# Sorting networks on VectorE: leaving idle lanes in their buffer instead of copying them at every step

## The chip, the cores and the metric

The kernel runs on one core of one Trainium2 chip. The metric is the device time of one execution in microseconds (us); lower is better. The engines are named as in the profile: PE (TensorE), DVE (VectorE), ACT (ScalarE), POOL (GpSimd) and SP (SyncE, which issues transfers).

## The reference

Sixteen graphs of 1024 nodes with 64 channels go through four layers, each with a layer norm and a ReLU ahead and a residual behind: a dense graph product, an attention layer, a hyperbolic attention layer, and a last layer that matters here. Cut to that:

```python
nd = adj_d > 0                                   # neighbours left after a thinning of the graph
vals = jnp.where(nd[..., None], x[:, None, :, :], jnp.inf)
s = jnp.sort(vals, axis=2)                       # per node and channel, over the neighbours
nv = nd.sum(2)
for tau, w in zip((0.25, 0.5, 0.75), (0.25, 0.5, 0.25)):
    pos = tau * maximum(nv - 1, 0)
    lo, hi, frac = floor(pos), ceil(pos), pos - floor(pos)
    agg = agg + w * (s[lo] + frac * (s[hi] - s[lo]))
out = x + agg
y = (relu(out @ W1 + b1) @ W2 + b2) * mask
```

So for each node and channel a weighted sum of three quantiles over the node's neighbours is wanted, which takes a sort of a few to some 288 values per node and channel.

## The kernel before, in words

The nodes of a graph are ranked by how many neighbours they have. The 80 with the most are **hubs**. They are sorted with channels (of two nodes at a time) on the 128 partitions and all their neighbours side by side in one row of 2736 values, cut into segments of 288, 192, 128, 96, 64, 48 and 40 lanes (`HUB`, `HUB_OFF`). The others, **lows**, have a node on each partition and 31 to 7 neighbours of 64 channels each in the row (`LOW`, seven groups per graph). Both sort by a Batcher network of comparators: a step takes the maximum and the minimum of pairs of lanes at a distance `k`, two DVE instructions for each regular set of pairs.

A step doesn't work in place. It reads one buffer and writes the other: `ha` and `hb` for the hubs, `la` (where gathered rows land) and `lb` for the lows. The next step swaps them. A lane that no comparator of a step touches, an idle lane, is therefore copied from one to the other by ACT, so that the next step finds all its lanes in one place. In `step` and `first` (hubs) the idle lanes come from `comparators`; in `sort_low` they are the set `stay` that `network` gives for each step. `lanes` and `at` make the strided views, `stretches` turns a set of lanes into regular runs.

`sort_hub` calls `step` for the networks of width 2, 4, 8, 16, 32 on all segments at once, then for the wider merges on the longer segments alone, with `first` where a segment isn't a power of two. `finish_hub` runs the sort and then multiplies the sorted lanes by weights that pick the quantiles and adds them up (`aggh`). `lows` does the same for each group (`aggl`).

What runs beside it are several Python generators, one for each kind of work: `heads` (layers 0 to 2 and the norm of layer 3), `places` (the thinning and the ranking: activations `d`, comparisons `rem`, casts `ng` and `vr`), `weigh`, `fetches` (the search for neighbours and the gathers by POOL into `la` and `hg`), `hubs`, `lows` and `finish`. A planner in Python (`Plan`, `Stream`) books a cost for every instruction, keeps a due time per generator from DVE time (`HEADS_US`, `HUBS_US`, `LOWS_US`) and picks whose next piece is emitted. The class `Queue` then fixes the order on every engine: each engine runs its instructions exactly in the order in which they were emitted, and a later one never overtakes one that waits. Nearly every instruction carries line 187 in the profile, the line of that helper, so groups are told apart by tile names.

Of the kernel before, what the change touches and what calls it, by code (L numbers as in the profile page):

```python
# [57 lines left out]
HUB_OFF = {}  # L58
# [200 lines left out]
def network(d, needed):  # L259


    out = []
    for st in reversed(batcher(d)):
        act = [c for c in st if needed & set(c)]
        both = {e for c in act for e in c}
        stay = needed - both
        out.append((st[0][1] - st[0][0], [a for a, _ in act if a in needed], [b for _, b in act if b in needed], stay))
        needed = stay | both
    assert needed == set(range(d))
    return out[::-1]  # L270
# [23 lines left out]
def tile_gnn_stack(  # L294
# [1525 lines left out]
    def comparators(D, p, k):  # L1820


        if k == p:
            runs = [(0, 1, D - p)]
        else:
            full = max(0, (D - 2 * k) // (2 * k) + 1) if D >= 2 * k else 0
            full = min(full, p // k - 1)
            while full and k + 2 * k * (full - 1) + 2 * k > D:
                full -= 1
            runs = [(k, full, k)] if full else []  # L1830
            part = D - (k + 2 * k * full) - k
            if full < p // k - 1 and part > 0:
                runs.append((k + 2 * k * full, 1, min(part, k)))
        used = set()
        for j0, m, w in runs:
            for g in range(m):
                for i in range(w):
                    used |= {j0 + 2 * k * g + i, j0 + 2 * k * g + i + k}
        idle, j = [], 0
        while j < D:  # L1840
            e = j
            while e < D and e not in used:
                e += 1
            if e > j:
                idle.append((j, e))
            j = max(e, j + 1)
        return runs, idle

    def lanes(buf, off, n, st, j, m, w, step):

        v = buf[:, off + j:off + j + n * st].rearrange("p (n d) -> p n d", d=st)
        if m == 1:
            return v[:, :, 0:w]
        return v[:, :, 0:m * step].rearrange("p n (m s) -> p n m s", s=step)[:, :, :, 0:w]

    def compare(hi, lo, a, b):
        nc.vector.tensor_tensor(hi, a, b, ALU.max)
        nc.vector.tensor_tensor(lo, a, b, ALU.min)

    def step(src, dst, p, k, blocks):  # L1860


        for so, do, n, st, D in blocks:
            idle = comparators(D, p, k)[1]
            if len(idle) == 2 and idle[0][1] - idle[0][0] == idle[1][1] - idle[1][0] and idle[1][0] <= st // 2:
                idle = [(*idle[0], 2, idle[1][0] - idle[0][0])]
            for j, e, *r in idle:
                m, stp = r or (1, 0)
                nc.scalar.copy(lanes(dst, do, n, st, j, m, e - j, stp), lanes(src, so, n, st, j, m, e - j, stp))
        for so, do, n, st, D in blocks:  # L1870
            for j, m, w in comparators(D, p, k)[0]:
                a, b = (lanes(src, so, n, st, j + o, m, w, 2 * k) for o in (0, k))
                for o, op in ((0, ALU.max), (k, ALU.min)):
                    nc.vector.tensor_tensor(lanes(dst, do, n, st, j + o, m, w, 2 * k), a, b, op)
                    yield []

    def first(dst, a, b, n, p, D):

        r = D - p
        av, bv = lanes(*a[:2], n, a[2], 0, 1, p, 0), lanes(*b[:2], n, b[2], 0, 1, r, 0)  # L1880
        dv = lanes(*dst[:2], n, dst[2], 0, 1, D, 0)
        compare(dv[:, :, 0:r], dv[:, :, p:D], av[:, :, 0:r], bv)
        if r < p:
            nc.scalar.copy(dv[:, :, r:p], av[:, :, r:p])

    def same(o, n, d, D=None):
        return (o, o, n, d, D or d)
# [1 line left out]
    def sort_low(a, b, pn, nt, d, needed):  # L1889

        def at(buf, j, m, st, w):
            v = buf[:pn].rearrange("p t l c -> p t (l c)")
            if m == 1:
                return v[:, :, j * C:(j + w) * C]
            o = j if j + m * st <= d else j - (st - w)
            assert o >= 0
            return v[:, :, o * C:(o + m * st) * C].rearrange("p t (m s) -> p t m s", m=m)[:, :, :, (j - o) * C:(j - o + w) * C]

        def parts(lanes, *offs):
            for j, m, st, w in stretches(lanes):  # L1900
                fits = m == 1 or all(j + o + m * st <= d or j + o >= st - w for o in offs)
                yield from [(j, m, st, w)] if fits else [(j, m - 1, st, w), (j + (m - 1) * st, 1, w, w)]

        for k, hi, lo, stay in network(d, set(needed)):
            for j, *r in parts(hi, 0, k):
                nc.vector.tensor_tensor(at(b, j, *r), at(a, j, *r), at(a, j + k, *r), ALU.max)
            for j, *r in parts(lo, 0, -k):
                nc.vector.tensor_tensor(at(b, j, *r), at(a, j - k, *r), at(a, j, *r), ALU.min)
            for j, *r in parts(stay, 0):
                nc.scalar.copy(at(b, j, *r), at(a, j, *r))  # L1910
            a, b = b, a
            yield
        return a

    def sort_hub(a, b):

        o40, o48, o64, o192, o128, o288, o96 = (HUB_OFF[c] for c in HUB_ORDER)
        s, d = a, b
        n40, n48 = (next(h[1] for h in HUB if h[2] == c) for c in (40, 48))
        for p in (1, 2, 4, 8, 16):  # L1920
            k = p
            while k:
                if p < 8:
                    yield from step(s, d, p, k, [same(0, HUB_N // (2 * p), 2 * p)])
                elif p < 16:
                    yield from step(s, d, p, k, [same(o40 + 16 * h, n40, 40, 16) for h in range(2)] + [same(o48, (HUB_N - o48) // 16, 16)])
                else:
                    yield from step(s, d, p, k, [same(o40, n40, 40, 32), same(o48, n48, 48, 32), same(o64, (HUB_N - o64) // 32, 32)])
                s, d, k = d, s, k // 2
                yield  # L1930
        first((a, o40, 40), (b, o40, 40), (a, o40 + 32, 40), n40, 32, 40)
        first((a, o48, 48), (b, o48, 48), (a, o48 + 32, 48), n48, 32, 48)
        n64 = (HUB_N - o64 - 6 * 96) // 64
        yield from step(b, a, 32, 32, [same(o64, n64, 64), same(o96, 6, 96, 64)])
        s, d, k = a, b, 16
        while k:
            yield
            yield from step(s, d, 32, k, [same(o40, n40, 40), same(o48, n48, 48), same(o64, n64, 64), same(o96, 6, 96, 64)])
            s, d, k = d, s, k // 2
        k = 64  # L1940
        while k:
            yield
            yield from step(s, d, 64, k, [same(o192, 1, 192, 128), same(o128, 4, 128), same(o96, 6, 96)])
            s, d, k = d, s, k // 2
        yield
        first((b, o192, 192), (a, o192, 192), (b, o192 + 128, 192), 1, 128, 192)
        yield from step(a, b, 128, 128, [same(o288, 1, 288, 256)])
        s, d, k = b, a, 64
        while k:
            yield  # L1950
            yield from step(s, d, 128, k, [same(o192, 1, 192), same(o288, 1, 288, 256)])
            s, d, k = d, s, k // 2
        yield
        first((b, o288, 288), (a, o288, 288), (b, o288 + 256, 288), 1, 256, 288)
        s, d, k = b, a, 128
        while k:
            yield
            yield from step(s, d, 256, k, [same(o288, 1, 288)])
            s, d, k = d, s, k // 2

    class Tail:
# [224 lines left out]
        def finish_hub(self, graph, a, b, wd):  # L2186
            wp = self.wp
            aggh = self.sums[graph, 0] = self.bp.tile([P, HQ], F32, name="aggh", bufs=2)
            yield from sort_hub(a, b)
            w = wp.tile([P, HUB_N], F16, tag="wb", name="wb", bufs=1)  # L2190
            for h in range(2):
                nc.sync.dma_start(w[64 * h:64 * h + 64, :], wd[h].partition_broadcast(64))
            yield
            yield [w]
            for q0, nq, cap, few in HUB:
                o, l0, l1 = HUB_OFF[cap], (few - 1) // 4, -(-3 * (cap - 1) // 4) + 1
                v, wv = (u[:, o:o + nq * cap].rearrange("p (n l) -> p n l", l=cap)[:, :, l0:l1]
                         for u in (a if cap in (192, 128, 96) else b, w))
                nc.vector.tensor_tensor(v, v, wv, ALU.mult)
                nc.vector.tensor_reduce(aggh[:, q0:q0 + nq], v, AX.X, ALU.add)  # L2200
            yield []
# [202 lines left out]
```

## Time and profile before

| what | value |
|---|---|
| runs of the kernel | 5921.93, 5931.84, 5931.37 us, median 5931.37 us |
| profiled execution | 6619.39 us, span 6617.5 us |
| mean granted TensorE clock in the profiled execution | 0.61 |
| DVE busy | 5113.9 us, 13,854 instructions in the record |
| ACT busy | 3432.8 us, 10,163 instructions |
| POOL busy | 3586.6 us, 2,903 instructions |
| PE busy | 3205.6 us, 13,232 matmuls |
| hub sort on DVE, `hb<-ha` and `ha<-hb` | 640.9 + 606.8 us, 1632 + 1568 instructions |
| low sort on DVE, `lb<-la` and `la<-lb` | 677.6 + 695.4 us, 1760 + 1856 instructions |
| copies of idle lanes on ACT, hubs | 273.2 + 255.8 us, 1280 + 1264 instructions |
| copies of idle lanes on ACT, lows | 300.5 + 223.3 us, 944 + 768 instructions |

The profile is of one execution, which took longer than the unprofiled runs; busy times and waits in it are compared with its own span. A group's row gives the tile written, the tile read, the number of instructions, their busy time and the mean of one, and then the engine's idle time ahead of them with what ended it. "PE granted clock" is a mean over the span. Some matmul records can be missing.

### The profile page before, as it was taken

The page shows a single profiled execution, that of the slowest core. Times are in us where ns is not written, and L with a number is a line of the kernel's source. Part 1 is how long each engine was busy: PE and PEld are TensorE (multiplying, and loading weights), DVE is VectorE, ACT ScalarE, POOL GpSimd, SP SyncE. Part 2 cuts the span into 40 slices and gives each one's busy share as a digit, 9 for nine tenths or more (in the row PEclk, how much of TensorE's full clock was granted, in tenths as well). Part 3 has the DMA queues.
Part 4 walks back from the last instruction along what each step waited for, and adds up shares of the span by engine and source line. Part 5 has one row for each costly group of instructions (what it writes and reads, how often), then busy time and mean ns, then how long its engine had stood idle before and what let it go on. Part 6 is the DMA issues. An engine that isn't in the chain of part 4 may idle for free. (4 is left out here: it accounts for less than half of the span.)

```text
span 6617.5 us, 61215 instructions
## 1 busy us (share of the span) xinstructions
PE 3205.6 (48%) x13232; PEld 1794.6 (27%) x13233; DVE 5113.9 (77%) x13854; ACT 3432.8 (52%) x10163; POOL 3586.6 (54%) x2903
## 2 busy tenths in 40 slices
PE   6554463645636445453545635346363645535310
PEld 2223232322413223231322413224132332313200
DVE  3568687795978869787796878869687796877957
ACT  5355464554656455564554646455464654645523
POOL 0263564655546564664646646465564546646576
PEclk7656556566655656655566656656566566665655
DMA  2221322222222222322223222222222222222121
GB/s 65 80 55 51 83 58 69 63 78 62 60 70 67 65 57 57 92 55 61 64 56 84 61 62 71 66 61 58 79 60 73 56 68 73 62 59 71 42 42 19
DMA packets 460786, 419.44 MB, mean 63 GB/s; under 512 B 218067, under 2 KB 351667, under 8 KB 460404
## 3 DMA queue, kind: packets, MB, share of 16 engines
q1 hardware_dynamic: 353908, 295.94, 15.6%
q0 software_dynamic: 106496, 119.49, 9.1%
q14 instruction: 275, 2.25, 0.1%
q8 instruction: 107, 1.75, 0.1%
HBM read 363.99 MB, written 50.54 MB: 63 GB/s over the span
## 5 line engine op out<-in xcount | busy, mean ns | idle before, releaser
L187 POOL DMA_INDIRECT la<-s_hd,ix x1856 | 2364.3, 1274 | 2144.2 <-DVE ix L187 1067.8
L187 POOL DMA_INDIRECT hg<-s_hd,ix x768 | 949.6, 1236 | 358.9 <-issue 275.7
L187 DVE TENSOR_TENSOR lb<-la 128x128 f32<-128x128 f32 (+14 forms) x1760 | 677.6, 436 | 269.2 <-ACT la L187 181.9
L187 DVE TENSOR_TENSOR la<-lb 128x256 f32<-128x256 f32 (+11 forms) x1856 | 695.4, 430 | 133.3 <-ACT lb L187 99.5
L187 DVE TENSOR_TENSOR ha<-hb 128x64 f32<-128x64 f32 (+36 forms) x1568 | 606.8, 441 | 174.8 <-ACT hb L187 122.5
L187 DVE TENSOR_TENSOR hb<-ha 128x128 f32<-128x128 f32 (+36 forms) x1632 | 640.9, 447 | 91.0 <-ACT ha L187 67.0
L187 PE MATMUL pv<-wtile,krow 8*128 8x512 f16 x512 | 292.6, 572 | 597.5 <-ACT d L187 299.7
L187 PE MATMUL pw<-ident,u_z 128*128 128x128 f32 x1024 | 236.8, 376 | 463.0 <-DVE u_z L187 358.2
L187 ACT COPY lb<-la 128x64 f32<-128x64 f32 (+11 forms) x944 | 300.5, 354 | 219.2 <-issue 76.7
L187 PE MATMUL pm<-w,hn 128*65 128x128 f32 x2048 | 404.7, 380 | 6.8 <-DVE w L187 6.8
L187 PEld LDWEIGHTS <-ng 128*128 128x128 f16 x2048 | 169.5, 126 | 818.9 <-issue 818.9
L187 ACT ACTIVATE d<-pv,n_mid 128x512 f16<-128x512 f32 x256 | 174.0, 688 | 419.4 <-remote 261.1
L187 PEld LDWEIGHTS pm<-w,hn 128*65 128x65 f32 x2048 | 388.3, 210 | 10.0 <-DVE w L187 9.9
L187 PE MATMUL pd<-tab_r,tab_dist 67*128 67x512 f32 x512 | 373.6, 821 | 25.7 <-DVE u_g L187 18.0
L187 POOL DMA_INDIRECT s_vp<-vr,s_place x128 | 134.8, 1053 | 433.7 <-DVE c_sb L187 142.6
L187 ACT ACTIVATE u_g<-pd,gxc 128x512 f32<-128x512 f32 x256 | 174.1, 680 | 365.4 <-PE pd L187 199.2
L187 PE MATMUL pl<-tab_ll,tab_rl 66*128 66x512 f32 x512 | 360.8, 795 | 0.0
L187 PEld LDWEIGHTS pw<-ident,u_z 128*128 128x128 f32 x1024 | 170.8, 193 | 674.3 <-issue 593.4
L187 PE MATMUL pf<-vcol,one 128*1 128x3 f32 x32 | 3.1, 166 | 664.5 <-DVE vcol L187 664.5
L187 PE MATMUL pa<-adj,h 128*64 128x512 f32 x512 | 199.8, 909 | 251.2 <-DMA adj<-in_adjt 117.6
L187 ACT COPY ha<-hb 128x4 f32<-128x4 f32 (+22 forms) x1264 | 255.8, 269 | 123.6 <-DVE hb L187 101.5
L187 ACT COPY hb<-ha 128x32 f32<-128x32 f32 (+24 forms) x1280 | 273.2, 284 | 79.6 <-DVE ha L187 65.9
(342 smaller groups left out, 8647.0 us busy)
## 6 DMA issues: line engine op xcount, KB each, us to landing
adj<-in_adjt SPq DMA_DIRECT2D x384, 512.0 KB
la<-s_hd,ix POOLq DMA_INDIRECT x1856
row<-s_vp SPq DMA_DIRECT2D x112, 256.0 KB
hg<-s_hd,ix POOLq DMA_INDIRECT x768
wb<-wd SPq DMA_DIRECT2D x32, 342.0 KB
row<-s_vp SPq DMA_DIRECT2D x192, 28.0 KB
row<-s_vp SPq DMA_DIRECT2D x192, 24.0 KB
xa<-in_x SPq DMA_DIRECT2D x16, 256.0 KB
```

The source lines that it names most:

```text
L187: r = f(*a, **k)
```

## The change

All sorts keep a record of where each lane is. A lane that a step leaves alone stays in the buffer it is in. Where the next step that reads it reads the other buffer, it is copied, once, at the first step at which it is idle; where that step reads the same buffer, it isn't copied.

For the lows this is worked out in `sort_low` from the list of steps: `where` holds the buffer of each lane, `reads` the lanes that each step reads (the last entry being those wanted at the end). The copies are also emitted ahead of the step's comparators and no longer after them. For the hubs a new class `Sort` with one instance `hs` does it in two passes: the first time, `sort_hub` runs with buffers named 0 and 1 and only records reads, writes and idle lanes (`touch`, `leave`); `search` goes through the record backwards to find what each idle lane is wanted in next, and forwards to make the list of copies for each call of `leave`; later runs of `sort_hub` emit these copies. A former merging of two equal idle stretches into one copy is gone from `step`; the new list merges by `stretches`. The comparators are unchanged, as are the constants of the planner.

```diff
@@ in the kernel's body, ahead of step @@
+    class Sort:
...
+        log, found, n = [], None, 0
+        def touch(self, kind, buf, off, n, st, j0, m, w, stp):
+            self.log.append((kind, buf, {off + st * q + j0 + stp * g + i for q in range(n) for g in range(m) for i in range(w)}))
+        def leave(self, src, dst, off, n, st, j, e):
+            if self.found is None:
+                self.log.append(("leave", src, dst, off, n, st, j, e))
+                return
+            for o, m, *r in self.found[self.n]:
+                nc.scalar.copy(lanes(dst, o, m, st, *r), lanes(src, o, m, st, *r))
+            self.n += 1
+        def search(self, final):
+            ahead, wanted = dict(final), []
+            for kind, *r in reversed(self.log):
...
+                else:
+                    for i in r[1]:
+                        ahead[i] = r[0] if kind == "read" else None
+            where, found = [0] * HUB_N, []
+            for kind, *r in self.log:
...
+                        which = [i for i in range(j, e) if want[o + i] == dst and where[o + i] == src]
+                        for i in which:
+                            where[o + i] = dst
...
+    hs = Sort()
@@ step @@
-            idle = comparators(D, p, k)[1]
-            if len(idle) == 2 and idle[0][1] - idle[0][0] == idle[1][1] - idle[1][0] and idle[1][0] <= st // 2:
-                idle = [(*idle[0], 2, idle[1][0] - idle[0][0])]
-            for j, e, *r in idle:
-                m, stp = r or (1, 0)
-                nc.scalar.copy(lanes(dst, do, n, st, j, m, e - j, stp), lanes(src, so, n, st, j, m, e - j, stp))
+            for j, e in comparators(D, p, k)[1]:
+                hs.leave(src, dst, so, n, st, j, e)
@@ first @@
+        if r < p:
+            hs.leave(a[0], dst[0], a[1], n, a[2], r, p)
...
-        if r < p:
-            nc.scalar.copy(dv[:, :, r:p], av[:, :, r:p])
@@ sort_low @@
-        for k, hi, lo, stay in network(d, set(needed)):
+        steps = network(d, set(needed))
+        reads = [{j for h in hi for j in (h, h + k)} | {j for l in lo for j in (l - k, l)} for k, hi, lo, _ in steps] + [set(needed)]
+        where = {j: 0 for j in range(d)}
+        for i, (k, hi, lo, stay) in enumerate(steps):
+            moved = []
+            for j in sorted(stay):
+                then = next(t for t in range(i + 1, len(reads)) if j in reads[t])
+                if where[j] == i % 2 and then % 2 != i % 2:
+                    moved.append(j)
+                    where[j] = 1 - i % 2
+            for j, *r in parts(moved, 0):
+                nc.scalar.copy(at(b, j, *r), at(a, j, *r))
             for j, *r in parts(hi, 0, k):
                 nc.vector.tensor_tensor(at(b, j, *r), at(a, j, *r), at(a, j + k, *r), ALU.max)
             for j, *r in parts(lo, 0, -k):
                 nc.vector.tensor_tensor(at(b, j, *r), at(a, j - k, *r), at(a, j, *r), ALU.min)
-            for j, *r in parts(stay, 0):
-                nc.scalar.copy(at(b, j, *r), at(a, j, *r))
+            for j in (*hi, *lo):
+                where[j] = 1 - i % 2
             a, b = b, a
             yield
@@ finish_hub @@
+            if hs.found is None:
+                for _ in sort_hub(0, 1):
+                    pass
+                hs.search({...})        # the lanes and buffers that the weighting reads at the end
+            hs.n = 0
             yield from sort_hub(a, b)
```

More of the change, by code (lines that the diff above doesn't have):

```diff
@@ L1858, in compare @@
         nc.vector.tensor_tensor(lo, a, b, ALU.min)
+    class Sort:
[12 more added lines that the diff above has]
+            for kind, *r in reversed(self.log):
+                if kind == "leave":
+                    src, dst, off, n, st, j, e = r
+                    wanted.append({i: ahead.get(i) for q in range(n) for i in range(off + st * q + j, off + st * q + e)})
+                else:
[3 more added lines that the diff above has]
+            for kind, *r in self.log:
+                if kind == "read":
+                    assert all(where[i] == r[0] for i in r[1])
+                elif kind == "write":
+                    for i in r[1]:
+                        where[i] = r[0]
+                else:
+                    src, dst, off, n, st, j, e = r
+                    want, runs = wanted.pop(), []
+                    for q in range(n):
+                        o = off + st * q
+                        which = [i for i in range(j, e) if want[o + i] == dst and where[o + i] == src]
+                        for i in which:
+                            where[o + i] = dst
+                        if runs and runs[-1][2] == which:
+                            runs[-1][1] += 1
+                        else:
+                            runs.append([o, 1, which])
+                    found.append([])
+                    for o, m, which in runs:
+                        for i, g, stp, w in stretches(which):
+                            parts = [(i, g, w, stp)] if g == 1 or i + g * stp <= st else [(i + stp * x, 1, w, 0) for x in range(g)]
+                            found[-1] += [(o, m, *p) for p in parts]
+            assert all(where[i] == b for i, b in final.items())
+            self.found = found
@@ L1870, in step @@
         for so, do, n, st, D in blocks:
             for j, m, w in comparators(D, p, k)[0]:
+                if hs.found is None:
+                    for o in (0, k):
+                        hs.touch("read", src, so, n, st, j + o, m, w, 2 * k)
+                    for o in (0, k):
+                        hs.touch("write", dst, so, n, st, j + o, m, w, 2 * k)
+                    continue
                 a, b = (lanes(src, so, n, st, j + o, m, w, 2 * k) for o in (0, k))
@@ L1879, in first @@
         r = D - p
+        if r < p:
+            hs.leave(a[0], dst[0], a[1], n, a[2], r, p)
+        if hs.found is None:
+            hs.touch("read", *a[:2], n, a[2], 0, 1, r, 0)
+            hs.touch("read", *b[:2], n, b[2], 0, 1, r, 0)
+            hs.touch("write", *dst[:2], n, dst[2], 0, 1, r, 0)
+            hs.touch("write", *dst[:2], n, dst[2], p, 1, r, 0)
+            return
         av, bv = lanes(*a[:2], n, a[2], 0, 1, p, 0), lanes(*b[:2], n, b[2], 0, 1, r, 0)
@@ L2188, in finish_hub @@
             aggh = self.sums[graph, 0] = self.bp.tile([P, HQ], F32, name="aggh", bufs=2)
+            if hs.found is None:
+                for _ in sort_hub(0, 1):
+                    pass
+                hs.search({HUB_OFF[cap] + cap * q + l: 0 if cap in (192, 128, 96) else 1 for q0, nq, cap, few in HUB
+                           for q in range(nq) for l in range((few - 1) // 4, -(-3 * (cap - 1) // 4) + 1)})
+            hs.n = 0
             yield from sort_hub(a, b)
```

## The prediction

> **What bounds the kernel now.** I read the busy line of the profile page first, then the groups of VectorE (DVE), then who waited for whom, and last the timeline of one long gap.
>
> ```profile
> span 6617.5 us, 61215 instructions
> ...
> PE 3205.6 (48%) x13232; PEld 1794.6 (27%) x13233; DVE 5113.9 (77%) x13854; ACT 3432.8 (52%) x10163; POOL 3586.6 (54%) x2903
> ```
>
> DVE is the fullest engine and its instructions stand in an order fixed when the program is built, so an idle microsecond on it is a microsecond of the run unless the next instruction waits for the same thing. Adding up DVE's idle stretches over the whole timeline gives 1373 us; 901 us of them end at an instruction of ScalarE (ACT). POOL, next in share, mostly waits for DVE (its gathers wait 1067.8 us for `ix`), so it would follow a faster DVE.
>
> The waits that the change touches are those of sorting instructions on the sorts' own copies:
>
> ```profile
> DVE lb L187 <- ACT la L187: 181.9, 58, 22.7
> DVE ha L187 <- ACT hb L187: 122.5, 7, 23.1
> DVE la L187 <- ACT lb L187: 99.5, 69, 16.4
> ...
> DVE hb L187 <- ACT ha L187: 69.1, 27, 9.8
> ```
>
> (total, times, longest; the buffer named after ACT is the one its copy wrote.) Summed by releaser over sorting instructions alone, this is 281.6 us in the neighbour sorts (la, lb) and 213.8 us in the hub sorts (ha, hb): 495 us. The longest column warns that this isn't the price of the copies, which take 0.2 to 1.1 us each. The timeline at the 23.1 us wait shows what it is, ACT first, then DVE:
>
> ```profile
> 3119.36 0.69 ACT L187 ACTIVATE d<-pv,n_mid 128x512 f16<-128x512 f32 x1 [9.79 <-remote]
> 3131.95 0.69 ACT L187 ACTIVATE d<-pv,n_mid 128x512 f16<-128x512 f32 x1 [11.91 <-remote]
> 3132.54 0.50 ACT L187 COPY la<-lb 128x384 f32<-128x384 f32 x1
> 3132.94 0.47 ACT L187 COPY hb<-ha 128x2 f32<-128x2 f32 x4
> ```
>
> ```profile
> 3133.26 0.43 DVE L187 TENSOR_TENSOR ha<-hb 128x95 f32<-128x95 f32 x2 [23.14 <-ACT hb L187]
> 3133.60 0.48 DVE L187 TENSOR_SCALAR rem<-d,n_ske 128x1024 f16<-128x1024 f16 x1
> ```
>
> A small copy stands on ACT's queue behind two `d` activations that themselves wait for something the trace calls remote. DVE is named as waiting for the copy, but 0.34 us later in its own order comes `rem<-d`, which needs the second `d`. With the copy gone DVE would stop there instead. So I split the 495 us: 282 us lie inside remote waits of ACT, and only 94 us (neighbour) and 40 us (hub) belong to waits that touch none. ACT's remote waits add up to 699 us, and the profiled run is 6619.39 us against a median of 5931.37; whether the unprofiled runs have these stalls no view tells.
>
> **What the Trainium skill says.** "ScalarE: Activation LUTs", section "What ACT_TABLE_LOAD costs", prices an ACT instruction with immediate operands at 186 ns + 0.833 ns per element, and says that two in a row overlap by about 93 ns. The trace agrees for contiguous copies: 240 ns at 64 elements, 508 ns at 384. It doesn't agree for strided ones (839 ns for 342 elements that lie eight apart), which the page doesn't treat. "Perfetto Trace Analysis", section "Optimization Strategy", says to take the engine one optimizes for, find its gaps and ask what updates the awaited semaphore; the case above shows that the named instruction may be innocent and the head of its queue guilty.
>
> **The change, part by part.**
>
> 1. Copies removed. The order of the built programs has 2544 hub copies before and 1440 after, and 1712 and 1104 in the neighbour sorts; by shape, 217 and 91 thousand elements per partition in the hubs, 314 and 142 thousand in the neighbours. The page's rows give 255.8 + 273.2 = 529 us for the hubs' copies and, with 223.3 us for `la<-lb`, 300.5 + 223.3 = 524 us for the neighbours'. At 0.85 ns per element that leaves 0.135 us per hub copy and 0.150 us per neighbour copy. After: 1440 x 0.135 + 77 = 272 and 1104 x 0.150 + 121 = 287. ACT sheds 1053 - 559 = 494 us, from 3433 to about 2940. None of that counts by itself: ACT has slack.
>
> 2. DVE's work. The same 16,341 instructions stand in DVE's order before and after, with the same shapes. Zero.
>
> 3. DVE's waits on sort copies. A lane idle for five steps was copied five times, each copy needing the one before it; now it is copied once, at the first idle step, or never. In the built order the sorting instructions of the hubs that carry an ACT semaphore fall from 849 to 294 (to 35%), those of the neighbours from 854 to 579 (to 68%). Applied to the waits outside remote stalls: 40 x 0.65 = 26 and 94 x 0.32 = 30. Of the 282 us inside remote stalls I take 20: about 1 us for each of some 20 long gaps, as `rem<-d` or `ex<-d` follows within about a microsecond. Bounds: 0 and half of it, 140. Sum 76.
>
> 4. ACT's other customers. DVE waits 221 us, outside remote stalls, for other ACT results in its non-sorting work (`ex`, `u_g`, `ln_v`, `rem`), and 33 us in the sorts. Their queue is 494/3433 = 14% lighter: 254 x 0.14 = 36. Bounds: 0, if they wait for PE anyway, and 90.
>
> 5. Bursts. The remaining copies come together. A hub sort goes from 37 groups of at most 9 copies to 13 groups, the largest of 26, 18, 15 and 10, with single lanes in pieces. A new group of 12 at one step (four pieces for each of three blocks) takes by the rows about 2.2 us; the four copies of that step took 1.5 us, and DVE's comparators there take about 1.9 us. The next step may wait some 0.5 us where nothing else is interleaved, and whatever stands behind the burst on ACT (`d`, `ng`, `hs`, `ex`) is pushed back as much; `rem` and `ex` on DVE wait for those. Four such groups per graph, 16 graphs: 64 x 0.5 = 32 lost. Bounds: 0 and 128 (2 us each).
>
> 6. Order. In the neighbour sorts copies now stand ahead of the step's comparators. They read what the previous step left, so they start no later. More first copies wait directly for gathered rows (672 with a DMA wait, 544 before); what queues behind such a copy is all of ACT, and the only row for it is 50.9 us in 3 waits before, so I leave it at nothing, with 20 as a bad end. The planner that writes the queues books fewer ACT instructions and interleaves differently: its two-graph rhythm (839 and 829 DVE instructions) becomes an even 834 in the second half. SP's and POOL's transfers are the same ones in slightly shifted places, hidden by DVE's work between; if that cover failed, a late gather such as the 17.3 us one before a `lb` is the price. Zero, plus or minus 40.
>
> Sum in the profiled run: 76 + 36 - 32 = 80 us of 6617. The unprofiled run is 10% shorter and may lack the stalls, so I drop the 20 us there: 60 us, or 5871.
>
> **Rivals.**
> *A, the long stalls go too (15%).* If the work DVE can reach without a copy is longer than in the gap shown, half of the 282 us goes: 60 + 140 = 200 faster, 5731. For it: hub streams have further steps ready. Against it: the written order puts `rem` and `ex` right behind.
> *B, the bursts cost more than the waits they replace (21%).* Its place is ACT's queue at the first idle step of each merge: `d`, `ng` and `ex` stand behind 12 or more pieces and DVE behind them. At 2 us for each of 64 bursts, 128 lost against 60 + 32 = 92 us gained without bursts gives 36 slower, 5967. It decides from 92/64 = 1.4 us per burst. For it: ACT's 901 us share of DVE's idle time. Against it: the steps after a burst have no copies.
> *C, the waits only change their name (10%).* DVE stops at `rem`, `ex` or `u_g` instead, even in the short waits: 0 to 12 us, about 5925. For it: the gap shown. That the copies don't fall in number is excluded by the built order.
>
> **How the numbers follow.** The forecast, 54%, is 5871. Without B and C the time falls by the sum's bounds: from 5850 to 5915 for the forecast itself, down to 5731 for A, up to 5967 for B. The range 5770 to 5965 leaves out most of A and the worst of B. A measurement of this kernel can tell about 0.2%, 12 us, from no change; faster 54 + 15 = 69%, same 10% from C, slower 21% from B.
>
> **What would show it.** Right: ACT busy near 2940 us; DVE busy within 1% of 5114; waits of `ha` and `hb` on ACT copies down to a third once remote stalls are set aside, those of `la` and `lb` to two thirds; 20 us gaps still there, now ahead of `rem`, `d` or `ex`. Wrong: DVE's idle time on ACT unchanged with new names (C); more waits on ACT `d`, `ex`, `u_g` behind runs of twelve copies (B); the long gaps gone (A).

## The result and the profile after

The changed kernel takes 5913.46 us (median of 20 runs) against 5933.66 us of the kernel before (median of 20 runs in turn with it): a ratio of 0.9965, 95% interval 0.9952 to 0.9979. It is faster by 0.35%, about 20 us. The forecast was 5871 us, 60 us faster, so the direction held and the forecast gain was three times too large.

The profile of before ahead of the prediction, with a span of 6617.5 us, is of an execution some 11% longer than the others, and all executions of the last set of runs below, those of before included, were about as long, so each ratio is to runs of before on the same chip in the same set. A second profile of before (the run before_again) has a span of 5917.3 us and none of ACT's waits on something remote; it is the one to set beside the profile after.

The first page of the profile after, span and busy times:

```profile
span 5922.9 us, 58834 instructions
...
PE 3205.7 (54%) x13232; PEld 1792.7 (30%) x13233; DVE 5110.1 (86%) x13854; ACT 3032.4 (51%) x8451; POOL 3773.5 (64%) x2903
```

Against the first page of before ACT lost 1712 instructions and 400 us; DVE's work is the same to 4 us. Who waited for whom on DVE, the kernel after (total, times, longest, in us):

```profile
DVE ln_v L187 <- ACT h L187: 86.2, 29, 5.5
...
DVE ymf L187 <- DMA ymu<-in_maskc: 64.9, 8, 12.6
DVE lb L187 <- DMA la<-s_hd,ix: 56.0, 5, 22.3
DVE la L187 <- ACT lb L187: 55.7, 52, 8.1
DVE lb L187 <- ACT la L187: 52.3, 23, 8.1
...
DVE hb L187 <- ACT ha L187: 22.5, 5, 14.8
...
DVE ha L187 <- ACT hb L187: 4.7, 4, 3.2
```

The same view of the second profile of before:

```profile
DVE la L187 <- ACT lb L187: 86.9, 64, 13.9
DVE ymf L187 <- DMA ymu<-in_maskc: 75.0, 13, 6.7
DVE ng L187 <- DMA adj<-in_adjt: 69.6, 22, 7.7
DVE ln_v L187 <- ACT h L187: 61.8, 33, 4.4
DVE lb L187 <- ACT la L187: 43.5, 43, 5.7
DVE hb L187 <- ACT ha L187: 41.8, 17, 15.0
DVE lb L187 <- DMA la<-s_hd,ix: 39.7, 5, 13.0
```

Summed by releaser over the timelines, sorting instructions waited 172.7 us for ACT's writes to the sort buffers before and 135.0 us after (hubs 42.3 and 27.1, neighbours 130.4 and 107.9). Not all of this is copies of idle lanes. ACT also fills `ha` with gathered hub rows that PE has transposed (`ha<-pg`, 96 instructions before and after), and the list by names puts both under `ha`. The view of the tile `pg` tells who waited for these rows, before_again first, then after:

```profile
L187 ACT COPY ha<-pg x96: 751/1077/1123, 354.9 to 5754.6; 128x512 f32<-128x512 f32 x64, 128x344 f32<-128x344 f32 x32
...
  DVE hb L187: 36.8, 9
```

```profile
  DVE hb L187: 22.5, 5
```

So idle lanes of the hubs were waited for 5.5 us before and 4.7 us after, and idle lanes of all sorts 136 and 113 us. DVE's whole idle time is 676 us before and 682 us after in these two executions; the execution of after that was profiled (5925.28 us) is one of its slower ones. Two rows in the lists have nothing to do with the copies: DVE waits for the node mask `ymu` and for gathered rows `la`. Both lead back to POOL, as the experiments show for the mask.

### The profile page after: what moved, and what is told of

Same layout as the page of the kernel before. It is cut to its first block, busy times and chain, and to the rows that moved or that the text cites. A ratio compares the mean times of both kernels' runs of the same rounds, so it can differ in the third digit from the quotient of the medians.

```text
span 5922.9 us, 58834 instructions
## 1 busy us (share of the span) xinstructions
PE 3205.7 (54%) x13232; PEld 1792.7 (30%) x13233; DVE 5110.1 (86%) x13854; ACT 3032.4 (51%) x8451; POOL 3773.5 (64%) x2903
## 3 DMA queue, kind: packets, MB, share of 16 engines
q8 instruction: 107, 1.75, 0.1%
## 5 line engine op out<-in xcount | busy, mean ns | idle before, releaser
L187 POOL DMA_INDIRECT la<-s_hd,ix x1856 | 2421.5, 1305 | 1398.2 <-DVE ix L187 737.7
L187 POOL DMA_INDIRECT hg<-s_hd,ix x768 | 1040.3, 1355 | 234.0 <-issue 207.8
L187 DVE TENSOR_TENSOR hb<-ha 128x128 f32<-128x128 f32 (+36 forms) x1632 | 640.8, 449 | 25.7 <-ACT ha L187 22.5
L187 POOL DMA_INDIRECT s_vp<-vr,s_place x128 | 164.4, 1285 | 433.9 <-DVE c_sb L187 140.7
L187 ACT COPY lb<-la 128x64 f32<-128x64 f32 (+6 forms) x784 | 195.1, 297 | 258.2 <-DVE la L187 90.0
L187 PE MATMUL pv<-wt,ng 128*128 128x128 f16 x2048 | 299.2, 298 | 0.0
L187 DVE FIND_INDEX8 ix<-seek,row 128x8 uint32<-128x1056 f16 x224 | 279.7, 1250 | 0.0
```

The costliest lines, as they stand in the source:

```text
L187: r = f(*a, **k)
```

## The experiments

These theories stood against each other after the result. **P**: the copies do free DVE, but POOL's chain of gathers and scatters is the next limit, and DVE meets it through PE's transposes `pg`, through SP's loads and directly. **B**: the bunched copies cost ACT's other customers what the sorts gain. **C**, that removed waits only change their name, is B's or P's weaker form. **R**, in the first runs, has the copies gain and the planner's new sequence give most of it back. A later one, **Q**, says that the copies are worth nothing in any sequence of the whole computation. **S** and A' are about the long execution alone.

The planner writes a different order for the new copies, so copies and order change together. To part them, the sequence in which the planner picks its streams was written down for one kernel and replayed in another. Both kernels have the same 11,895 steps:

```diff
-        while fetch.live or any(o.live for o in others):
...
-                (fetch if fetch in ready else min(ready, key=lambda o: o.due)).step(now)
+        streams = [fetch, *others]
+        for i in WRITTEN:              # the number of the stream, 11,895 of them
...
+            streams[i].step(0.0)
```

The orders of DVE, PE, SP and POOL are then those of the kernel that the sequence comes from, instruction for instruction; only ACT's copies differ. In the traces PE, SP, POOL and the rest of ACT agree in every record, DVE in all but 18 of 13,854 or fewer. Two parts of the change stay together in all these runs: that there are fewer copies, and that in the neighbour sorts they stand ahead of the step's comparators.

### before_again: the kernel before, unchanged

> The kernel before, profiled once more. Theory S (the stalls of ACT on something remote, 699 us in the first profile of before and none in the profile of after, belong to that one profiled execution): the span comes out at 5920 to 5950 us, ACT's remote waits near 0, DVE idle time near 690 us (5930 less about 5240), with sorting instructions waiting for sort copies about 130 to 200 us. Theory A' (the copies of before bring the stalls about): the span is again near 6600 us and the remote waits near 700 us.

The span was 5917.3 us, ACT's remote waits 0 and DVE's idle time 676 us, as theory S had it (its span was to begin 3 us higher). The 700 us of stalls belonged to the long execution and not to the copies of before: in after_again, with the new copies, they are back. What is behind them stays open.

### new_copies_old_order and old_copies_new_order: copies and sequence apart

> The new copies, but the streams are stepped in the sequence that the planner wrote for the kernel before: the orders of DVE, PE, SP and POOL are those of before instruction for instruction, only ACT's copies differ. Theory R (the copies gain, the planner's new sequence gives most of it back, 65 us of it where the mask load ymu stands on SP behind nvr): 50 to 80 us faster than before, 5855 to 5885, no wait of ymf. Theory C (removed waits only change their name): 0 to 25 us faster, about 5915, as the kernel after. Theory B (bursts cost): slower than the kernel after.

> The old copies of all idle lanes, with the streams stepped in the sequence that the planner wrote for the kernel after: DVE, PE, SP and POOL as after. Theory R: slower than before by 30 to 60 us, 5965 to 5990, with ymf waiting some 65 us in total. Theory C: within 15 us of before.

Ratios to before, the last one from the 20 runs of the result:

| | sequence written for the old copies | sequence written for the new copies |
|---|---|---|
| old copies | 1 | 1.0020 (1.0014 to 1.0027) |
| new copies | 1.0065 (1.0051 to 1.0078) | 0.9965 (0.9952 to 0.9979) |

The last ratio comes from another set of runs than the other two. Theory R was wrong in both: in the old sequence the new copies are slower by 39 us (5957.57 against 5918.86), not faster by 50 to 80, and the old copies in the new sequence lose 13 us with a `ymf` wait of 1.1 us, not 30 to 60 with one of 65. The new copies alone can cost. But the sort waits did fall there, from 172.7 to 103.9 us, and in the new sequence from 251.5 to 135.0; the `ha<-pg` rows in these sums are 36.8, 48.9, 16.3 and 22.5 us. Where the time went in the old sequence is in the waits of DVE:

```profile
DVE xa L187 <- PE po L187: 110.7, 16, 18.3
DVE ymf L187 <- DMA ymu<-in_maskc: 73.2, 13, 6.8
```

`xa`, the end of layer 1, waited 27.0 us before and now waits in every one of the 16 graphs. The timeline at the 12 us wait, first PE, then DVE:

```profile
2861.21 0.60 PE L187 MATMUL pv<-wt,ng 128*128 128x128 f16 x4
2868.03 0.48 PE L187 MATMUL pg<-ident,hg 128*128 128x128 f32 x1 [6.21 <-DMA hg<-s_hd,ix]
2869.23 0.47 PE L187 MATMUL pg<-ident,hg 128*128 128x128 f32 x1 [0.72 <-DMA hg<-s_hd,ix]
2870.44 0.47 PE L187 MATMUL pg<-ident,hg 128*128 128x128 f32 x1 [0.74 <-DMA hg<-s_hd,ix]
2871.93 0.48 PE L187 MATMUL pg<-ident,hg 128*128 128x128 f32 x1 [1.01 <-DMA hg<-s_hd,ix]
...
2874.34 1.06 PE L187 MATMUL po<-ident,r 128*128 128x128 f32 x4
```

```profile
2875.44 0.69 DVE L187 TENSOR_TENSOR xa<-po,xb 128x512 f32<-128x512 f32 x1 [12.15 <-PE po L187]
```

The transposes of gathered hub rows stand ahead of `po` on PE, and they arrive one every 1.2 us or a little more, which is POOL's pace of issuing gathers there, 0.94 us busy and 0.30 us to the next. PE waits, then DVE. In this profile PE waits 185.8 us for `hg` in all, 128.7 us in before_again. My reading is that DVE had come to the place earlier than the sequence was written for, and POOL had not; the runs with fewer gathers below test it.

### after_mask_early: the mask load moved up on SP

```diff
+            mu = bp.tile([P, NT], U8, name="ymu")
+            nc.sync.dma_start(mu, maskc[...])     # beside hl and xl, at the start of finish
             ad = dp.tile([N, C], F32, name="ad")
             yield [aggh, aggl]
...
-            mu = bp.tile([P, NT], U8, name="ymu")
-            nc.sync.dma_start(mu, maskc[...])
             yield [mu, py]
```

> The kernel after, its sequence of streams kept, with the load of the mask ymu issued on SP at the start of finish, beside hl and xl, and so ahead of the nvr loads that wait for the scatter into s_vp. Theory R: the 64.9 us of ymf go and most of it is time, 5850 to 5875. Theory C: the 65 us turn up ahead of the next instruction on DVE that needs SP or ACT, 5900 to 5915.

It took 5874.92 us, 0.9915 of before (0.9895 to 0.9934), by the ratios some 25 to 30 us better than the kernel after, which is at the edge of what R gave and better than C did. The cause of the wait, in the kernel after, on SP's queue:

```profile
4344.55 1.75 SPq L187 DMA_DIRECT2D nvr<-s_vp  x4
4346.34 0.36 SPq L187 DMA_DIRECT2D ymu<-in_maskc  x1
```

and then on DVE:

```profile
4348.28 0.17 DVE L187 CAST ymf<-ymu 128x8 f32<-128x8 uint8 x1 [12.59 <-DMA ymu<-in_maskc]
```

A load of 1024 bytes stands behind `nvr`, which waits for POOL's scatter into `s_vp` (SP's waits for it add up to 1186.2 us in 16 stops). With the mask moved the 64.9 us of `ymf` are gone, but `nvi`, which needs `nvr` itself, now waits 57.8 us instead of 18.6. So about 40 of the 65 us come back one instruction later, at the same scatter. I had named this row as the doing of the new sequence; before_again has 75.0 us of it too. But the old copies in the new sequence have 1.1 us of it, so there it does come with the new copies.

### before_half, new_old_half, new_new_half: POOL with less to do

Here half of the hub gathers are left out:

```diff
-                    for l in range(8):
+                    for l in range(0, 8, 2):
                         fetch(g[:pn, l, h, :], ix, l, pn)
...
-                        nc.tensor.transpose(pg[:, l, 0:pn], g[:pn, l0 + l]...
+                        nc.tensor.transpose(pg[:, l, 0:pn], g[:pn, l0 + l - l % 2]...
```

> Half of the hub gathers are left out: of the eight lanes of a hub row only the even ones are gathered and stand for the odd ones too, so the hubs' result is not the reference's. Old copies, old sequence; DVE and SP order as before. It is the base for the next run. Theory P (POOL's chain of gathers and scatters is the next limit; it reaches DVE through PE's transposes pg, through SP's nvr loads and the mask load behind them): a little faster than before, 20 to 50 us, as 24 of 164 gathers of a graph, about 38 us of POOL, are gone and DVE's waits on ymf and xa shrink. Theory B (bursts of copies are what costs): within 10 us of before, since DVE is the limit.

> The same half of the hub gathers left out, with the new copies in the old sequence. Theory P: the 111 us of xa behind PE's pg fall below 30, and the new copies are now faster than before_half by about the 70 us of sort waits that they remove, at least by 40. Theory B: the new copies stay slower than before_half by some 40 us, as they were with all gathers.

> The same half of the hub gathers left out, new copies in the new sequence. Theory P: faster than the kernel after by 30 to 70 us, with the waits of ymf on the mask load below 20 us, since the scatter into s_vp leaves POOL earlier. Theory B: within 15 us of the kernel after.

All three ran on one chip. Old copies: 5726.64 us, 0.9682 of before (0.9669 to 0.9695). New copies in the same sequence: 5689.07 us, 0.9611 (0.9595 to 0.9628). New copies in the new sequence: 5748.07 us, 0.9719 (0.9706 to 0.9733).

Two things follow. POOL's gathers limit the kernel before far more than I had thought: the run loses 188 us when 384 of 2624 are dropped, where I expected 20 to 50. (Their transfers go too, and these runs don't part the issue on POOL from the transfer. 13 us of the 188 are DVE's busy time, the rest its idle time.) And the copies' effect in the old sequence turns round: 39 us slower with all gathers, 38 us faster with half of the hub ones, just under the 40 that P had set as the least. The waits of DVE, before_half first:

```profile
DVE la L187 <- ACT lb L187: 59.3, 67, 4.1
DVE lb L187 <- ACT la L187: 36.2, 38, 2.6
DVE xa L187 <- PE po L187: 23.3, 9, 7.5
```

new_old_half:

```profile
DVE xa L187 <- PE po L187: 37.5, 14, 7.5
DVE la L187 <- ACT lb L187: 29.4, 44, 3.4
...
DVE lb L187 <- ACT la L187: 15.9, 7, 2.7
```

The sorts' waits halve (112.8 to 55.5 us by the timeline) and `xa` keeps 37.5 us where it had 110.7. The 30 us bound I had set for it was missed by a little. B expected the 40 us loss to stay and falls as the sole cause of it: the bunches of copies are the same. new_new_half was expected 30 to 70 us faster than the kernel after and was faster by some 2.5%, more than twice that; its `ymf` waits are 0. It is also slower than the same copies in the old sequence, so a sequence has no value of its own: it fits one balance of engines.

### after_fetch, after_mask_fetch, after_mask_fetch175, before_mask_fetch: the planner told what a gather costs

`Plan.FETCH` is the planner's price for one gather on POOL's queue. The profiles of before_again and after show 1.28 to 1.36 us busy on average and 0.30 us to the next, so 1.6 us from one to the next, where the planner had 1.45 (the 0.27 and 1.55 us of the expectations below are misread):

```diff
-    HOP, FETCH, LAND, RATE = 0.06, 1.45, 2.2, 185e3
+    HOP, FETCH, LAND, RATE = 0.06, 1.6, 2.2, 185e3
```

after_fetch has this edit alone, the other two of after have the mask edit too (with 1.75 in after_mask_fetch175), and before_mask_fetch has both edits on the old copies. The planner is free.

> The whole computation: new copies, mask load at the start of finish, and the planner's price for POOL's issue of a gather raised from 1.45 to 1.6 us (the traces show 1.28 to 1.31 us busy and 0.27 us between two), with the planner free to write its own sequence. Theory P: 5840 to 5880, since the sequence then places what needs POOL later; the waits of nvi on nvr, 57.8 us with the mask load moved alone, shrink. Theory B has nothing to say on it: about as with the mask load moved, 5875.

> The kernel after with the planner's price of a gather issue at 1.6 us alone, the mask load where it was. Theory P: the sequence avoids part of the waits by itself; 5810 to 5880, the mask load still late by some 5 us in most graphs.

> As after_mask_fetch, with 1.75 us. Theory P: if the price matters since it is near what a gather costs, 1.75 overshoots the 1.55 us of the traces and gains no more: 5790 to 5860.

> The old copies with the two edits of after_mask_fetch: mask load at the start of finish, planner's price of a gather issue 1.6 us, planner free. It tells what the new copies are worth where POOL is planned for. Theory P: with POOL's chain less in the way the new copies keep most of the sort waits that they remove, so this kernel is 30 to 70 us slower than after_mask_fetch, 5830 to 5870. Theory Q (the gain of after_mask_fetch comes from the sequence alone and the copies are worth nothing in any sequence of the whole computation): within 15 us of 5800.

| kernel | us | ratio to before |
|---|---|---|
| after_mask_fetch | 5801.41 | 0.9804 (0.9790 to 0.9818) |
| after_fetch | 5824.51 | 0.9795 (0.9778 to 0.9812) |
| after_mask_fetch175 | 5846.64 | 0.9837 (0.9822 to 0.9853) |
| before_mask_fetch | 5834.73 | 0.9813 (0.9798 to 0.9828) |

after_mask_fetch was run on one chip and the other three on another, so their ratios and not their times are compared. One constant is worth 1.7% on the new copies (0.9795 against 0.9965), five times the change under study, and it makes the mask edit idle: after_fetch has 0.4 us of `ymf` wait left to remove. All four kernels planned with a higher price gain 1.6 to 2%, so it isn't one lucky sequence. after_fetch and after_mask_fetch can't be told apart; either beats both kernels. Theory P missed on before_mask_fetch, which I expected 30 to 70 us behind: the old copies reach the same ratio within the intervals, as Q said.

### new_old_mask: the mask early in the old sequence

> New copies in the old sequence, the mask load at the start of finish. With the sequence kept, its 73 us of ymf go. Theory P: since the same graphs also wait for PE's pg behind POOL (111 us at xa), part of the 73 us comes back there; 5900 to 5940, against 5958 with the mask load late.

The ratio is 1.0013 (1.0004 to 1.0021), against 1.0065 with the mask late. The 73.2 us of `ymf` are gone; this profile's DVE waits show where most of them are now:

```profile
DVE xa L187 <- PE po L187: 133.4, 16, 18.2
...
DVE nvi L187 <- DMA nvr<-s_vp: 41.7, 13, 4.0
```

22.7 us more at `xa`, 41.7 us at `nvi`: two other windows on POOL. Predicted in kind, and about half a per cent was kept. The time, 5951.95 us, lies above the 5900 to 5940 expected, on a chip where before took 5945 us and not 5919; by the ratio it would lie inside.

### Two sequences with the price of 1.6, each with both kinds of copies

Sequence A is that of after_mask_fetch, sequence B that of before_mask_fetch. Each was replayed with the other copies.

> Old copies in the sequence of after_mask_fetch. Theory P: slower than after_mask_fetch (0.9804) by 20 to 60 us, 0.984 to 0.991 of before. Theory Q: 0.980 within 0.002.

> New copies in the sequence of before_mask_fetch (DVE, PE, SP and POOL in its order). Theory P, with POOL the next limit wherever DVE runs ahead: between 0.974 and 0.983 of before, at most 40 us faster than before_mask_fetch (0.9813). Theory Q (worth nothing): 0.981 within 0.002.

old_copies_seq_a: 1.0031 of before (1.0020 to 1.0041), against 0.9804 for the new copies in the same sequence. That is 2.3%, more than twice what P allowed, and Q falls with it. Its sorting instructions wait 218.0 us for copies where after_mask_fetch has 97.3. new_copies_seq_b: 0.9830 (0.9816 to 0.9843) against 0.9813, nothing to tell; but its profile showed DVE idle for 563 us and that of before_mask_fetch 608. Since the two ran on different chips they were run once more on one:

> before_mask_fetch once more, on the chip of the next run: old copies in sequence B. 0.978 to 0.985 of before by either theory.

> New copies in sequence B. Theory P (the copies gain where POOL has room): faster than the run above by 25 to 55 us, as the profiled spans and DVE's idle time (563 against 608 us) say. Theory Q (worth nothing in a sequence of the whole computation that wasn't written for them): within 12 us of it.

> The kernel after on the same chip: 0.995 to 0.998 of before by either theory.

In this set before took 6613.06 us, old copies in sequence B 6440.24 us (0.973, interval 0.9698 to 0.9762), new copies 6346.23 us (0.9593, 0.9557 to 0.9630), the kernel after 6540.19 us (0.9895, 0.9861 to 0.9929). By the ratios the new copies gain about 90 us in sequence B, more than either theory allowed, and between before and after 73 us, 1% where 0.2 to 0.5% was expected. In the earlier set, with executions of about 5800 us, sequence B had shown no gain. So the pair doesn't settle the copies' worth at that length; the two sets also differ in the chip, and which of the two matters isn't known.

## Why the prediction was right and wrong

**The sum of the copies (step 1) and DVE's work (step 2) held.** ACT's copies fell from 1053 to 555.7 us (157.7 + 121.8 + 195.1 + 81.1), where 559 was worked out. Counts and shapes carried this far. ACT's busy time fell only to 3032 us and not to 2940, since the row of a group counts time in which another group is busy too: in the trace of before_again ACT is busy for 3428 us, and for 2592 us without the copies, so that all four groups hold 836 us of their own and not 1053.

**The split of the waits held in the total.** 134 us of waits outside remote stalls had been called the genuine part; the second profile of before shows 172.7 us, and none of the stalls (in the first one they add up to 717 us, where 699 is written). The hub part of it was misread: of the 40 us outside stalls 26.8 are waits for `ha<-pg`, which no copy of an idle lane causes. In after_again, as long as the first profile of before, the long gaps stand ahead of `ex` and `rem`, as said:

```profile
DVE ex L187 <- ACT ex L187: 178.9, 22, 17.7
DVE rem L187 <- ACT d L187: 95.0, 17, 18.9
```

Rival A, the stalls going too, is excluded by them. The sum for executions of this length, 80 us of 6617, was nearly measured, 73 us of 6613. That is the total alone: waits on sort copies fell from 495 to 190 us between the two profiles of this length, and those of DVE's other work on ACT rose from 364 to 526 us.

**Step 3, sort waits: too small in a fixed sequence, too large in the free one.** 56 us were put on these waits outside stalls. With the sequence held they fall by 69 us (old) and 116 us (new), and those for idle lanes alone by 81 and 122 us; but the planner's new sequence starts from more, 251.5 us, so that between before and after only 38 us are gone, 23 of them for idle lanes. The 26 us set for the hubs had 5.5 us to draw on. In item 6 of the parts I had allowed the new sequence plus or minus 40 and taken zero; it costs 13 us with the old copies. That the direction held is in part luck: in the sequence written for before the same copies lose 39 us.

**Step 4 had the wrong sign.** A lighter ACT was to save 36 us on its other results. Those waits of DVE's non-sorting work, 202.4 us in before_again, are 241.9 us in the kernel after, 39.5 us more. With the sequence held they change by +12 (old), +29 (new), -0.5 (A) and +5 us (B): in none of four sequences did a lighter ACT shorten them by as much as 1 us. POOL isn't behind it, as new_new_half, with fewer gathers, still has 239.5 us. Nor are bursts of copies (step 5): inside these 241.9 us ACT spends 4.9 us on sort copies. In the largest of them, 86.2 us at `ln_v`, ACT runs the very instructions that are waited for, `h`, about 4 us for one group, and `d` ahead of them. DVE reaches such places earlier and meets the same work of ACT; that it is this and nothing more is my reading. The 32 us set for bursts thus have no counterpart here, and that bursts decided the loss in the old sequence doesn't fit new_old_half.

**The step that failed beside it is the reading of POOL**: "it would follow a faster DVE", and in step 6 its transfers "hidden by DVE's work between", at zero. From 1067.8 us of POOL waiting for `ix` I took that POOL had slack. It has it in one place of nearly every graph: in before_again 15 waits of 45 to 61 us, one about every 354 us, make up nearly all of the 807.2 us.

```profile
POOL la L187 <- DVE ix L187: 807.2, 20, 60.7
POOL la L187 <- issue: 486.7, 1597, 0.3
```

Between, gather mostly follows gather after 0.3 us, and a faster DVE runs into the end of that. In the new sequence DVE's waits on transfers rise from 135.4 us (old copies) to 236.4 us (new copies), of which `ymf` is 64.9; in the old sequence they hardly move and those on PE rise from 64 to 149 us instead. With a sequence held, that is where most of what the sorts gained went, and the dropped gathers, turning a loss of 39 us into a gain of 38 us, show it for the old sequence. For the new one there is no such pair; the mask edit, which got back 25 to 30 us behind POOL's scatter, points the same way. Between before and after, where the sequence changes too, waits on transfers rise by 27 us and those on PE fall by 16, and step 4 is the larger miss. What the planner's sequence trades for what is not taken apart further.

**Scaling by leaving out** was the last fault. Going from the long execution to the usual one I took off only the stalls, as if the rest of the timeline were the same. Without stalls DVE is 86% busy instead of 77%, and POOL's waits for `ix` shrink from 1067.8 to 807.2 us.

## What to carry to other kernels

Idle time of a second engine that is gathered in one long wait per period is no slack for the rest of the period: before taking time off the first engine, drop part of the second engine's work and see what the run loses. Where an order is written by a planner, replay one written sequence with both versions, or the order's luck will be taken for the change's worth. And a planner's price that is a tenth too low (1.45 us where the trace has 1.6) can matter more than the work it schedules.

## What the runs showed of the hardware

How long a gather on POOL takes goes with what DVE does beside it. Sort the 2624 gathers of before_again by the DVE instructions that cover most of each one. The 196 with an idle DVE take 0.97 us on average, and the 110 beside `w<-pw,adj`, which has one input in PSUM, 0.95 us. Beside comparators, with both inputs in SBUF, the averages are 1.28 us (`la<-lb`), 1.40 (`lb<-la` and `hb<-ha`) and 2.11 (`ha<-hb`). A few long ones make up much of that: the medians are 0.94 us for the first two groups and 1.03, 1.29, 1.03 and 1.20 us for the comparators. The Trainium skill, "SBUF — State Buffer", section "Who interferes with whom", says that a DVE instruction with two SBUF inputs contends with a GpSimd instruction that reads SBUF, while one with a single SBUF input, outside the faster modes that use two ports, doesn't. These rows agree with it, but not all do: beside the hub weighting (`hb<-hb,wb` and `ha<-ha,wb`), also with both inputs in SBUF, 49 gathers take 0.97 us. No run here changed DVE's instructions to test it. With the new copies in the old sequence the neighbours' gathers grew longer, 1321 ns on average against 1283:

```profile
L187 POOL DMA_INDIRECT la<-s_hd,ix x1856 | 2452.2, 1321 | 1432.5 <-DVE ix L187 778.4
```

That would be 70 us of POOL's time for a DVE that sorts more densely, but the averages differ by more between the runs (1260 to 1376 ns), so it isn't shown to be the copies' doing.
